# Moving the last eight query steps of the fourth batch from the second attention slot to the first

## The chip, the cores and the metric

The kernel runs on one core of a Trainium2 chip. The metric is the device time of one execution in microseconds (us), lower is better. In the texts PE is TensorE (matmuls), PEld its loading of weights, DVE is VectorE, ACT is ScalarE, POOL is GpSimd, and SP is SyncE, whose queue issues nearly all transfers (DMAs). In the profile's counts one matmul instruction on fp32 data appears as two records.

## The reference

One pre-normalised transformer block on fp32 data: 4 batches of 512 tokens, width 512, 32 query heads and 8 key/value heads of 16 columns, and a gated MLP of width 1376.

```python
x = L0_attn_resid                                   # (4, 512, 512)
x = x + _L0_attn_ref(_layernorm(x, axis=-1), Wq, Wk, Wv, Wo)
x = x + _L0_ffn_ref(_layernorm(x, axis=-1), W_gate, W_up, W_down)

# _L0_attn_ref
q = rope(resid @ Wq); k = rope(resid @ Wk); v = resid @ Wv      # rope: q*cos + rotate_half(q)*sin
att = where(causal, q @ k.T / 4, -inf); probs = softmax(att)
return concat_heads(probs @ v) @ Wo
# _L0_ffn_ref
return (silu(x @ W_gate.T) * (x @ W_up.T)) @ W_down.T
```

## The kernel before

**Groups and slots.** Attention is done in 32 groups, one for each batch, block of 8 heads (m = 0 to 3) and half of it (4 heads at a time). Eight groups make the slot of one batch: `slot(b, steps)` runs groups 8b to 8b + 7. `steps` is a list of other PE work, each entry with a planned cost, that is woven between the attention's products ("fill"). In the first slot the fill is the query, key and value projections of batches 1, 2 and 3. In the second slot it is what is left of batch 3's projections, then batch 0's output projection, LayerNorm and MLP. Slots three and four carry the later batches' MLPs.

**A group.** A group g has four visits (n = 0 to 3) and a last visit. In each visit PE makes score products of two kinds (lines 1014 and 1027): scores of group g + 2 in plain order, of which DVE takes the greatest of each row (`greatest`, line 1060, which writes the tile `low`), and scores of group g the other way round, of which ACT takes exponentials (line 1115). POOL zeroes what lies above the diagonal (`causal`, line 1120). PE may write the next visit's scores only after DVE and ACT have read this visit's. After the visits `last_visit` makes the last scores, ACT two exponentials, POOL two causal masks, and then POOL makes the masked queries of group g + 3 (`masked`, line 999). `averages` (line 1142) multiplies the exponentials with the values. The next group's first score products read a tile that line 999 writes.

**What fills the gaps.** After a visit's `greatest`, the call `odd_steps` lets DVE do small pieces that are due (rotations, transposes), and `gap(n)` then lets PE do fill steps up to a share of the slot's total: `part += total * shares[n] / 8`, and `fill` takes steps as long as half of the next one's cost still fits. In the first slot `shares` has four entries that matter, one for each visit.

**Projections.** `projected` makes a block of 128 rows by 512 tokens from 8 steps, one for each half of the tokens and each quarter of the depth: 4 instructions of 32 columns by 256 tokens (line 305), planned at 0.43 us. Steps 1 to 4 use tokens 0 to 255, steps 5 to 8 the others. `rest3` lists batch 3's 48 steps: keys 8, queries of block 0 8, values 8, queries of blocks 1, 2, 3 with 8 each. In the first slot ACT copies a finished block out of PSUM (line 357) and DVE and POOL rotate the copy: shuffle (line 364) and cosine product (line 368) on DVE, sine product (line 365) and sum (line 369) on POOL. In the second slot DVE reads PSUM itself. A finished key block also gets a shuffle on DVE (line 428) and four products on POOL (line 431), the "spread".

**LayerNorm of batches 2 and 3.** Twelve passes on ACT for each batch (`calm`, kinds a, b, c: lines 238 and 239, 245, 407), one popped in each `odd_steps` unless POOL work is being held; that is four in a group of the first slot. After each b pass POOL runs three small instructions (lines 246 to 248). After each c pass of batch 3 the tile is flipped: DVE transposes blocks of it (line 320), SP stores it in four DMAs (line 324) and loads it back in order as one of four tiles of `xnT` (line 326). The load of tile i - 1 is issued behind the stores of tile i; the last two loads come behind the stores of tile 3. The second slot's first products of batch 3 read that `xnT`, those of batch 2 another.

**POOL's other work in the first slot** is two sums in each group that prepare MLP weights (line 646), the scaling of the averages (line 1166), and rotations. POOL runs its instructions in the order in which they were issued.

**The MLP of one batch** (`seven`) makes ten units of seven half-size products each. The first product's result is kept in `once` (line 696), which lies in the last columns of the sine table; an ACT copy (line 734) writes it.

Of the kernel before, what the change touches and what calls it, by code (L numbers as in the profile page):

```python
# [18 lines left out]
B, T, D = 4, 512, 512  # L19
NH, NKV, DH = 32, 8, 16  # L20
FF = 1376
P = 128
NT = T // P
NK = D // P
# [50 lines left out]
def preln_block_kernel(  # L75
# [57 lines left out]
    rope_sb = const.tile([P, 2 * T + 4], F32, name="rope_sb")  # L133
# [11 lines left out]
    homes = [const.tile([P, NF, T], F32, name=f"home{n}") for n in range(3)] + [wd_sb]  # L145
# [17 lines left out]
    whole = NF - 1  # L163
# [19 lines left out]
    thin = [True]  # L183
# [67 lines left out]
    calm = deque()  # L251
# [373 lines left out]
    def after(step):  # L625
        return 0.0, step
# [64 lines left out]
    def seven(b, n, blocks):  # L691


        x, home = xnTs[0], homes[n]
        rights = (x[:, 0:2, 0 : 2 * P], x[:, 2:4, 0 : 2 * P], x[:, 2:4, 2 * P :], *((sums if b else sums0)[s] for s in (3, 0, 1, 2)))
        once = rope_sb[:, 2 * NK * 96 : 2 * T]
        carried = deque()

        def owed():
            if carried:  # L700
                carried.popleft()()

        def product(ps, right, w):
            for k in range(2):
                product_of(ps, w[:, k, :], rights[right - 1][:, k, :], k == 0, k == 1)

        def halved(t):
            return t.rearrange("p (h t) -> p h t", h=2)

        def unit(u):  # L710
            v, a, f = b * whole + u, u % 2, 2 * (u // 2)
            left, right = slice(0, 2 * P), slice(2 * P, T)
            out = (u_sb if a else home[:, f : f + 2, :]).rearrange("p f t -> p (f t)")
            corners = out.rearrange("p (h t) -> p h t", h=4)[:, 0:4:3, :]
            ps = {}

            def twice(t):
                return t.unsqueeze(1).broadcast_to([P, 2, 2 * P])

            def ended():  # L720
                for which in (1, 0):
                    g, t = home[:, f + which, :], u_sb[:, which, :]
                    if a == 0:
                        nc.scalar.activation(t, g, AF.Tanh, scale=0.5)  # L724
                        carried.append(lambda g=g, t=t: nc.vector.scalar_tensor_tensor(g, t, 1.0, g, ALU.add, ALU.mult))
                    else:
                        engine = nc.gpsimd if narrow[0] else nc.vector
                        engine.tensor_tensor(g, g, t, ALU.mult)  # L728

            def a1():  # L730
                load_blocks("y", v + 1)
                ps["a"] = bank()
                product(ps["a"][:, left], 1, place("a", v)[:, 0])
                nc.scalar.copy(once, ps["a"][:, left])

            def y1():
                load_blocks("v", v + 1)
                load_blocks("a", v + 1)
                ps["y"] = bank()
                product(ps["y"][:, left], 2, place("y", v)[:, 0])  # L740
                owed()

            def y2():
                product(ps["y"][:, right], 6, place("y", v)[:, 1])
                nc.vector.tensor_tensor(halved(out[:, T:]), halved(ps["y"]), twice(once), ALU.add)

            def v1():
                load_blocks("w", v + 1)
                ps["v"] = bank()
                product(ps["v"][:, left], 7, place("v", v)[:, 0])  # L750
                owed()

            def v2():
                product(ps["v"][:, right], 5, place("v", v)[:, 1])
                nc.vector.tensor_tensor(corners, halved(ps["v"]), twice(out[:, 3 * T // 2 :]), ALU.add)
                nc.vector.tensor_tensor(out[:, right], ps["v"][:, right], out[:, left], ALU.add)

            def w1():
                ps["w"] = bank()
                product(ps["w"][:, left], 4, place("w", v)[:, 0])  # L760

            def w2():
                product(ps["w"][:, right], 3, place("w", v)[:, 1])
                joined()

            def first_w2():
                ps["w"] = bank()
                product(ps["w"][:, right], 3, place("w", v)[:, 1])

            def last_w1():  # L770
                product(ps["w"][:, left], 4, place("w", v)[:, 0])
                joined()

            def joined():
                nc.vector.tensor_tensor(corners, halved(ps["w"]), corners, ALU.add)  # L775
                ended()

            order = (a1, y1, y2, v1, v2, w1, w2) if v else (a1, y1, first_w2, y2, v1, v2, last_w1)
            return [(0.86, step) for step in order]

        steps = []
        for u in range(whole):
            steps += unit(u)
            if u % 2 and b > 0:
                steps.append(after(lambda p=u // 2: later_sums(b, n, p, (0, 1))))
        t = [after(lambda s=s: sums_of(s, b)) for s in range(4)]
        ends = edge(n)
        if b == 0:
            return [*steps[:1], t[2], *steps[1:2], t[3], *steps[2:], *ends], t[:2]
        steps[12:12] = [after(moved)]  # L790
        for cut, step in zip((44, 50, 56, 62, 66, 72), blocks):
            steps.insert(cut, after(step))
        return [ends[0], t[0], ends[1], t[1], ends[2], t[2], ends[3], t[3], *steps]
# [400 lines left out]
    begin3, turned3, rest3, _ = projections(3, 3)  # L1194
    begin2, turned2, rest2, load2 = projections(2, 2)
    begin1, turned1, rest1, _ = projections(1, 1, then=load2)
# [68 lines left out]
    def slot(b, steps):  # L1265

        steps = deque(steps)
        total = sum(cost for cost, _ in steps)
        done, part = 0.0, 0.0
        groups = range(8 * b, 8 * b + 8)  # L1270
        thin[0] = copied[0] = b == 0
        narrow[0] = True

        shares = (0.2, 0.225, 0.2875, 0.2875, 0.0) if thin[0] else (0.19, 0.19, 0.22, 0.22, 0.18)

        def upcoming(n):

            upto, us = part + total * shares[n] / 8, 0.0
            for cost, _ in steps:
                if done + us + cost / 2 > upto:  # L1280
                    break
                us += cost
            return us

        def gap(n):
            nonlocal done, part
            part += total * shares[n] / 8
            pool_steps(sums_at(g)[n])
            done = fill(steps, part, done)

        for g in groups:
            h = g + 2
            if thin[0]:
                laid_out(g + 1)
            for n, visit in enumerate(visits):
                e = (e0, e0, e1, e1)[n]
                if h < len(GROUPS):
                    both_scores(h, g, visit)
                    exponentials(e[:, slice(0, 2) if n % 2 else slice(2, 4), :], less)
                elif n % 2 == 0:  # L1300
                    both_scores(h, g, visit)
                    exponentials(e[:, 2:4, :], less)
                    exponentials(e[:, 0:2, :], plain)
                if n == 1:
                    causal(e0, 0)
                if n == 3:
                    causal(e1, 0)
                    causal(e1, 3 * P, exchanged=True)
                all_greatest(h, visit)
                holding[0] = n == 3  # L1310
                if thin[0]:
                    odd_steps((1.3, 0.95, 0.95, 1.05)[n], (2, 1, 1, 0)[n])
                else:
                    odd_steps(min(0.8 * upcoming(n) - (0.4, 0.4, 0.8, 0.8)[n], 2.3))
                gap(n)
                if n == 1 and not thin[0]:
                    laid_out(g + 1)
            last_visit(h, g)
            turned_round(h)
            averages(g)  # L1320
            odd_steps(1.4)
            if not thin[0]:
                gap(4)
        thin[0] = copied[0] = narrow[0] = False
        emptied(len(full))
        if b == B - 1:
            do(later, len(later))
        for cost, step in steps:
            step()
# [10 lines left out]
        nc.scalar.dma_start(out=homes[1], in_=spill)  # L1340

    turns = [step for pair in zip(turned2, *[iter(rest1[-8:])] * 2) for step in pair]
    early = [*rest1[16:-8], *turns, begin3, *rest2, *turned3, *rest3[:-24]]
    for u in range(whole):
        early.insert(4 * u + 4, after(lambda u=u: copies(u)))

# [43 lines left out]
    def timed(steps, asides):  # L1390
# [15 lines left out]
        after(pack_rest),  # L1406
        after(lambda: pool_steps(0)),
        *blocks,
        *rest3[-24:-12],
        *before[1:],  # L1410
        *rest3[-12:-2],
        *behind,
        rest3[-2],
        first_sums[0],
# [76 lines left out]
```

## Time and profile before

| | us |
|---|---|
| median of 3 runs (lowest, highest) | 838.42 (837.94, 839.71) |
| the profiled execution | 838.44 |
| its span in the profile | 836.6 |
| PE busy in the span | 815.5 (97%) |
| DVE, POOL, ACT busy | 567.6, 369.1, 233.5 |
| chain that ended last | PE 78%, DVE 13%, issue 2%, DMA 2%, POOL 2% |

The chain that ended last is followed back from the last instruction, and its shares say which engine the end waited for. The first slot's group 0 ends at 65.62 us, groups 1 to 7 take from there to 173.64, and the second slot runs from 173.64 to 347.86. A group of the first slot takes 15.15 to 15.30 us, but for group 4 with 16.62 us. TensorE was granted its full clock in all of them (1.00 in the windows).

### The profile page before, as it was taken

Reading aid. Unit: us, or ns where it says so; the run is one execution under the profiler, and the core shown is the slowest. Engines: PE = TensorE matmul, PEld = TensorE weight load, DVE = VectorE, ACT = ScalarE, POOL = GpSimd, SP = SyncE. Lnnn points to the kernel's source line nnn. Section 1 sums busy time; section 2 is a strip of 40 time slices with the busy share of each in tenths; the row PEclk is TensorE's granted clock in tenths of the full one; section 3 lists DMA queues with packets and bytes.
Section 4 is the critical chain, followed back from the end, with each engine's and each line's share of the span. In section 5 each row is a group of like instructions: output and inputs, shape, how many; then the busy total and the mean of one; then the engine's idle time right before and its main releaser. Section 6 shows DMA issues by size and latency. Waiting matters only on the chain.

```text
span 836.6 us, 29336 instructions
## 1 busy us (share of the span) xinstructions
PE 815.5 (97%) x12460; PEld 469.6 (56%) x12460; DVE 567.6 (68%) x1635; ACT 233.5 (28%) x352; POOL 369.1 (44%) x524
## 2 busy tenths in 40 slices
PE   6999999999999999999999999999999999999998
PEld 5664454443555554333655555446555556788887
DVE  7976777878977774467777775687776633656632
ACT  1045654432323232122233332222332330011100
POOL 4576685873866333122365534522244435101130
PEclk9999999999999999999999999999999999999999
DMA  7544324152577640234244532234334434545901
GB/s 213 116 118 116 92 67 90 57 173 45 176 238 259 200 161 7 75 144 90 86 156 154 186 105 98 84 81 117 96 107 129 136 115 140 128 141 173 297 32 50
DMA packets 147857, 105.57 MB, mean 126 GB/s; under 512 B 60208, under 2 KB 133936, under 8 KB 147600
## 3 DMA queue, kind: packets, MB, share of 16 engines
q1 hardware_dynamic: 147008, 97.94, 39.8%
q10 hardware_dynamic: 720, 5.77, 1.7%
q8 instruction: 98, 1.61, 0.8%
q14 instruction: 31, 0.25, 0.1%
HBM read 82.25 MB, written 25.17 MB: 128 GB/s over the span
## 4 chain that ended last, share of the span: by engine, by line
PE 78%; DVE 13%; issue 2%; DMA 2%; POOL 2%; SPq 1%; ACT 1%; POOLq 0%; DVEq 0%; ACTq 0%
PE mm L305 38%; PE mm L302 15%; PE sc L1014 12%; DVE junk L1060 7%; PE av L1142 6%; PE sc L1027 4%; PE mm L596 2%; PE mm L588 1%; DVE st L222 1%; POOL e L1120 1%; DVE rot L364 1%; PE mm L310 1%; POOL qa L999 1%; DMA xa<-in_x 1%; ACT e L1115 1%
## 5 line engine op out<-in xcount | busy, mean ns | idle before, releaser
L1060 DVE CUSTOM_DVE_ANT_0 junk<-sc,mask 128x128 f32<-128x128 f32 (+3 forms) x512 | 251.1, 490 | 127.7 <-PE sc L1027 65.9
L1115 ACT ACTIVATE e<-sc 128x1024 f32<-128x1024 f32 (+1 forms) x192 | 165.5, 881 | 370.1 <-PE sc L1027 274.5
L305 PE MATMUL mm<-xnT,shared 128*32 128x256 f32 x3632 | 216.7, 381 | 0.0
L1120 POOL TENSOR_SCALAR_AFFINE_SELECT e<-e 128x512 f32<-128x512 f32 (+2 forms) x192 | 106.1, 562 | 198.2 <-ACT e L1115 195.2
L305 PEld LDWEIGHTS mm<-xnT,shared 128*32 128x32 f32 x3632 | 121.2, 110 | 86.1 <-issue 24.5
L1014 PE MATMUL sc<-home,qa 32*64 32x512 f32 (+6 forms) x2048 | 157.0, 421 | 6.4 <-DVE low L1060 3.2
L1027 PE MATMUL sc<-qa,home 32*64 32x512 f32 (+6 forms) x2048 | 152.4, 427 | 1.5 <-DVE low L1060 0.8
L1014 PEld LDWEIGHTS sc<-home,qa 32*64 32x64 f32 x2048 | 67.1, 131 | 82.3 <-DVE low L1060 29.3
L1142 PE MATMUL av<-e,home 128*32 128x512 f32 (+3 forms) x1024 | 82.6, 438 | 2.5 <-POOL e L1120 2.4
L302 PE MATMUL mm<-xnT,shared 128*128 128x256 f32 x360 | 80.2, 383 | 0.0
L302 PEld LDWEIGHTS mm<-xnT,shared 128*128 128x128 f32 x360 | 68.5, 192 | 11.6 <-issue 2.2
L305 PE MATMUL mm<-wd_sb,home 128*32 128x256 f32 (+3 forms) x848 | 71.2, 470 | 0.0
L1027 PEld LDWEIGHTS sc<-qa,home 32*64 32x64 f32 x2048 | 58.9, 130 | 20.9 <-DVE low L1060 7.2
L1142 PEld LDWEIGHTS av<-e,home 128*32 128x32 f32 x1024 | 30.6, 109 | 48.3 <-issue 35.0
L728 POOL TENSOR_TENSOR home<-home,u 128x512 f32<-128x512 f32 x30 | 37.9, 1282 | 28.4 <-DVE u L775 28.4
L305 PEld LDWEIGHTS mm<-wd_sb,home 128*32 128x32 f32 (+1 forms) x848 | 28.0, 110 | 36.9 <-issue 27.4
L305 PE MATMUL mm<-wo_sb,cx 128*32 128x512 f32 x384 | 45.4, 595 | 0.0
L818 POOL TENSOR_TENSOR wd_sb<-home 128x256 f32<-128x256 f32 x15 | 10.9, 729 | 74.4 <-DVE home L728 74.1
L1060 DVE DVE_READ_ACCUMULATOR2_ANT low<- 128x1 f32 x512 | 42.4, 83 | 0.0
L1166 POOL TENSOR_TENSOR inv<-us,inverse 128x256 f32<-128x256 f32 x32 | 21.7, 678 | 44.2 <-DVE inverse L1159 44.0
L724 ACT ACTIVATE u<-home 128x512 f32<-128x512 f32 x40 | 23.0, 622 | 62.9 <-DVE home L775 51.8
L225 POOL TENSOR_TENSOR rstd<-rstd,neghalf 128x1 f32<-128x1 f32 x24 | 15.6, 648 | 55.6 <-DVE rstd L224 55.6
(152 smaller groups left out, 928.4 us busy)
## 6 DMA issues: line engine op xcount, KB each, us to landing
shared<-packed SPq DMA_DIRECT2D x118, 256.0 KB
flip<-u SPq DMA_DIRECT2D x88, 64.0 KB
shared<-packed SPq DMA_DIRECT2D x40, 128.0 KB
xnT<-flip SPq DMA_DIRECT2D x18, 256.0 KB
wd_sb<-differences SPq DMA_DIRECT2D x7, 640.0 KB
rows<-in_x SPq DMA_DIRECT2D x14, 256.0 KB
out<-rows SPq DMA_DIRECT2D x13, 256.0 KB
xa<-in_x SPq DMA_DIRECT2D x12, 256.0 KB
```

Source lines behind the costliest of these rows:

```text
L302: nc.tensor.matmul(out, lhsT=lhsT, rhs=rhs, start=start, stop=stop)
L305: nc.tensor.matmul(out[c : c + 32], lhsT=lhsT[:, c : c + 32], rhs=rhs, start=start, stop=stop)
L596: nc.tensor.matmul(ps[96:P, ts(q, P)], lhsT=rest_w[:, a, kq, 32 * q : 32 * q + 32], rhs=xnTs[0][:, kq, most:], start=kq == 0, stop=kq == N ...
L724: nc.scalar.activation(t, g, AF.Tanh, scale=0.5)
L728: engine.tensor_tensor(g, g, t, ALU.mult)
L1014: nc.tensor.matmul(dst[at : at + 64, :n], lhsT=qa[g][rows_of(r), q : q + 64], rhs=keys_of(g)[rows_of(r), :n], start=True, stop=True,)
L1027: nc.tensor.matmul(dst[at : at + 64, first_q:], lhsT=keys_of(g)[rows_of(r), k : k + 64], rhs=qa[g][rows_of(r), P * j + first_q :], start=True,
L1060: nc.vector.tensor_tensor_reduce(out=junk[:, :n], in0=src, in1=mask[:, T - n : T] if i else mask[:, T:], scale=-1.0, scalar=BIG, op0=ALU.a ...
L1115: nc.scalar.activation(dst, src, AF.Exp, scale=1.0 / math.sqrt(DH))
L1120: nc.gpsimd.affine_select(out=e[rows, heads, c : c + P], in_=e[rows, heads, c : c + P], compare_op=ALU.is_ge, fill=0.0, base=base, pattern ...
L1142: nc.tensor.matmul(av[32 * r : 32 * r + 32, P * j :], lhsT=v[:, j, 4 * (m // 2) + r, DH * (1 - hf) : DH * (3 - hf)], rhs=e[:, r, c : c + n ...
L1166: nc.gpsimd.tensor_tensor(us[m][:, :, hf, :], turned[0][:, :, hf, :], by, ALU.mult)
```

## The change

Four places change; everything else is the same.

```diff
-        once = rope_sb[:, 2 * NK * 96 : 2 * T]
+        once = rope_sb[:, 2 * NK * 96 : 2 * T] if b else homes[0][:, whole, : 2 * P]
...
-        shares = (0.2, 0.225, 0.2875, 0.2875, 0.0) if thin[0] else (0.19, 0.19, 0.22, 0.22, 0.18)
+        shares = (0.22, 0.256, 0.262, 0.262, 0.0) if thin[0] else (0.19, 0.19, 0.22, 0.22, 0.18)
...
                 if thin[0]:
+                    if calm and n == 1:
+                        calm.popleft()()
                     odd_steps((1.3, 0.95, 0.95, 1.05)[n], (2, 1, 1, 0)[n])
...
-    early = [*rest1[16:-8], *turns, begin3, *rest2, *turned3, *rest3[:-24]]
+    early = [*rest1[16:-8], *turns, begin3, *rest2, *turned3, *rest3[:-16]]
...
-        *rest3[-24:-12],
+        *rest3[-16:-10],
         *before[1:],
-        *rest3[-12:-2],
+        *rest3[-10:-2],
```

- The eight steps of batch 3's query block 1 (`rest3[-24:-16]`) go from the head of the second slot's list to the end of the first slot's. The remaining sixteen stand differently around batch 0's output projection: six before it and ten behind, where twelve and twelve stood.
- The first slot's fill is shared out anew: more in visits 0 and 1, less in visits 2 and 3.
- In visit 1 of each group of the first slot one more LayerNorm pass is popped, so that a group pops five.
- For batch 0's MLP the kept product lies in row 10 of `homes[0]` and no longer in the sine table.

## The prediction

> **What bounds the kernel now.** I read the page first (PE busy 97%, the chain of waits 78% PE), then the busy times by group, because the change moves work between two stretches.
>
> ```profile
> core 0: us, PE busy (x) PEld busy (x) DVE busy (x) ACT busy (x) POOL busy (x), PEclk, DMA share, GB/s
> 96.21:111.46 15.25, 14.57 (x288) 7.21 (x288) 10.96 (x41) 9.16 (x18) 11.35 (x17) 1.00 0.02 4
> 111.46:128.08 16.62, 15.05 (x312) 7.49 (x312) 12.73 (x45) 8.56 (x14) 13.55 (x23) 1.00 0.32 83
> 173.64:347.86 174.22, 172.65 (x2981) 87.20 (x2984) 127.07 (x379) 50.85 (x70) 89.08 (x118) 1.00 0.47 147
> ```
>
> Each row gives a stretch, its length, and the busy time of each engine. Groups 3 and 4 of the first slot leave PE 0.68 and 1.57 us idle; the whole second slot leaves 1.57 us in 174. So a PE step taken out of the second slot should shorten it by its own length, and a step put into the first slot is free only where PE idles. Where it idles is seen in the timeline of PE in group 3:
>
> ```profile
> 96.38 0.65 PE L1014 MATMUL sc<-home,qa 32*64 32x512 f32 x2 [0.17 <-POOL qa L999]
> ...
> 97.74 1.50 PE L305 MATMUL mm<-xnT,shared 128*32 128x256 f32 x24
> 99.34 0.65 PE L1014 MATMUL sc<-home,qa 32*64 32x512 f32 x2
> ...
> 100.39 1.50 PE L305 MATMUL mm<-xnT,shared 128*32 128x256 f32 x24
> 102.06 0.54 PE L1014 MATMUL sc<-home,qa 32*64 32x384 f32 x2 [0.17 <-DVE low L1060]
> ...
> 103.01 1.93 PE L305 MATMUL mm<-xnT,shared 128*32 128x256 f32 x32
> 105.07 0.54 PE L1014 MATMUL sc<-home,qa 32*64 32x384 f32 x2
> ```
>
> A row is start, length, line and what ended an idle time. Visits 0, 1 and 2 start at 96.38, 99.34 and 102.06, so they last 2.96, 2.72 and 3.01 (visit 3 also 3.01). Each ends when DVE has taken the greatest values. The fill of three steps (24 records, 1.50) or four (32, 1.93) is nearly done by then: a step is 0.43, and there is under 0.25 of room. The last stretch of a group hangs on POOL:
>
> ```profile
> 107.81 1.91 POOL L1120 TENSOR_SCALAR_AFFINE_SELECT e<-e 128x512 f32<-128x512 f32 x3
> 109.94 0.83 POOL L1120 TENSOR_SCALAR_AFFINE_SELECT e<-e 128x256 f32<-128x256 f32 x2 [0.22 <-ACT e L1115]
> 110.87 0.70 POOL L999 TENSOR_SCALAR qa<-home,rope_sb 128x512 f32<-128x512 f32 x1
> ```
> ```profile
> 121.68 1.52 POOL L431 TENSOR_SCALAR home<-kr,rope_sb 128x512 f32<-128x512 f32 x2
> 123.17 1.52 POOL L431 TENSOR_SCALAR home<-ks,rope_sb 128x512 f32<-128x512 f32 x2
> 124.64 2.75 POOL L1120 TENSOR_SCALAR_AFFINE_SELECT e<-e 128x512 f32<-128x512 f32 x5
> 127.50 0.69 POOL L999 TENSOR_SCALAR qa<-home,rope_sb 128x512 f32<-128x512 f32 x1
> ```
>
> The first is group 3, the second group 4. PE's last scores start at 108.08 and 123.28, the queries (L999) 2.79 and 4.22 later. In group 4 the key spread of batch 2 holds the masks back: 1.43 lost, which is why that group takes 16.62. Five masks take 2.75, so POOL must be free by 0.05 after the last scores start.
>
> **The change part by part.** The time is made against the profiled execution, 838.44, which is the median's 838.42 within 0.02. Which fill stands in which visit I counted in the built programs' order.
>
> *Second slot, steps removed.* Fills of 48 and 16 records there take 2.80 and 1.07, so four steps are 1.73 and eight are 3.46. Gain 3.46. Their DVE and POOL work hardly moves: the block finishes at the very end of the first slot, and its rotation lands in group 8. There one more cosine product (0.69) stands in front of the first greatest; visit 1 starts at 178.02, 0.11 behind DVE's end, so this costs some 0.5. In group 10 PE waited 0.19 for DVE and 0.41 for POOL's last masks; the two gate products that held these up (L728, 2.53) now stand a visit earlier: gain 0.5. I set the two against each other: 0 (bounds -0.7 to +1.0). The new place of `once` takes away one ACT wait of 2.4 us for POOL's sine product, but PE had other work and waited for nothing then: 0. PE idles 0.6 in groups 9 to 11 together, and the two waits of group 10 are all of it, so nothing is left to gain.
>
> *First slot, fill too long for its visit.* A fill starts 1.36 behind visit 0's start, 1.05 behind visit 1's, 0.95 behind the others', and the next scores start 0.07 before it ends. Four steps in visit 0 give 1.36 + 1.93 - 0.07 = 3.22 against 2.96: 0.26, in groups 1, 3 and 5: 0.78. Four steps in visit 1 give 2.91 against 2.72: 0.2, in group 6 (group 4 is counted below). Group 2 gets a transpose and three steps (2.09 to 2.23) in visit 1, where a transpose and two steps (1.66) stood: 3.14 against 2.73, 0.41, and 0.04 in visit 0; group 1's visit 2 gets the same pair, 3.11 against 3.01: 0.1. Four steps in visits 2 and 3 end at 2.81 of 3.01 and cost nothing. Group 0's longer visit 1 hides under that group's own POOL backlog (masks at 62.19, 0.6 behind its last scores); cover gone, 0.2. Sum 1.53 (1.1 to 1.9).
>
> *First slot, POOL.* The moved steps bring batch 3's LayerNorm and both key spreads forward. Group 4: after visit 1's start POOL now has a sine product (begins at 0.67, 1.80), a sum 1.27, a weight sum 0.73, a mask 0.64, a LayerNorm trio (104.53 to 105.80 in group 3, 1.3 with its gaps), the spread 3.0, another weight sum 0.73 and another trio 1.3 ahead of the masks: free at 11.5. The last scores come at 2.91 + 3.01 + 3.01 = 8.93. So the masks are 2.5 late, and the group takes 2.96 + 11.5 + 2.75 + 0.8 = 18.0 against 16.62: 1.4. Group 3: counted from visit 0's start, DVE's cosine product lets POOL's sum run 3.6 to 4.9, then weight sum to 5.6, mask 6.2, trio (behind ACT's pass) 7.75, sine product 9.05, weight sum 9.75, trio 11.1, key sum 12.4, with the last scores at 3.22 + 2.7 + 6.02 = 11.95: 0.4. Group 7 gets batch 3's spread, with no trio: 11.8 against 11.7, 0.1. Sum 1.9 (0 to 3.4). The fifth pass itself is 0.8 to 1.0 on ACT, whose exponential of visit 2 has 0.75 of slack: 0.
>
> On the sine product: its length in the trace is 1.27 to 1.81, long where a DVE cosine product (0.69) runs beside it.
>
> ```profile
> L365 POOL TENSOR_TENSOR rot<-rot,rope_sb x18: 1267/1288/1808, 37.0 to 215.9; 128x512 f32<-128x512 f32 x18
> ```
>
> The Trainium skill, SBUF — State Buffer, section "SBUF: two separate sides", says that VectorE with two SBUF inputs and GpSimd contend for one port pair as an exclusive lock, held for the whole instruction. The rows show 0.52 of lengthening beside an operation of 0.69, so nearly that; by the page group 4 would be 0.17 later still and the total as much higher, by the row it stays as summed.
>
> *First slot, a tile that is not there yet.* SP's timeline of the flips in group 5, and a load of such a tile in the chain of waits:
>
> ```profile
> 135.02 2.25 SPq L324 DMA_DIRECT2D flip<-u  x4
> 137.38 1.33 SPq L326 DMA_DIRECT2D xnT<-flip  x1
> 138.75 2.25 SPq L324 DMA_DIRECT2D flip<-u  x4
> 141.12 3.52 SPq L326 DMA_DIRECT2D xnT<-flip  x2
> ```
> ```profile
> 25.85 2.71 DMA wd_sb<-flip
> ```
>
> Before, batch 3's first key step came at 147.41 in group 6, ten us behind tile 1's load. Now it stands in visit 3 of group 5, while tile 2's flip is still the odd piece of visit 1, and tile 1's load is queued on SP behind tile 2's stores. From visit 2's start: transpose 0.71, stores 2.2 to 2.4, load 2.71, together 5.7. The step comes at 3.01 + 0.95 + 0.64 = 4.6. It waits 1.1, PE with all behind it, less 0.2 of room in the visit: 0.9. Lower bound 0 (a load that need not wait for its own stores may land sooner than the chain's), upper 1.9 (the load of 137.38 took 0.8 longer to issue). Tiles 2 and 3 are due after that wait and then just arrive.
>
> Sum: -3.46 + 0 + 1.53 + 1.9 + 0.9 = +0.9, so 839.3.
>
> **Rivals.** *POOL is later still (slower).* In groups 3, 4 and 7 POOL is the last; if there its sine products take 1.80 each (0.5 more in groups 3 and 7) and its weight sums 1.18, as the one at 152.69 did (0.45 more: once in group 3, twice in group 4), the POOL term is 2.4 larger: 841.7. It decides from the point where POOL is free 0.05 behind the last scores; for it speaks that POOL is busy 13.55 of 16.62 in group 4, against it that sums mostly take 0.73. *POOL is in time (faster).* The spread of batch 2 starts a visit earlier than before; if trios and sums find room in front of it, group 4 loses nothing and the old 1.43 goes: -3.46 + 1.53 - 1.4 + 0.9 = -2.4, 836.0. For it speaks that groups 5 and 6 carry two rotations and two weight sums and are in time (masks at 155.07, last scores at 155.10), against it the count above. *The second slot doesn't give the steps back.* Its weight sums, stores and loads run at a set number per group; if these hold the MLP's first units, half of 3.46 comes: 841.1. Against it: PE never waits for a load there.
>
> **How the numbers follow.** Chances: the forecast 0.38, POOL later 0.28, POOL in time 0.24, second slot 0.10. 0.2% (1.68 us) is about what a measurement of this kernel can tell from no change, so no change ends at 836.8 and 840.1. Of the forecast a quarter lies above 840.1 (its own range is 838.0 to 840.9) and 0.02 of it below 836.8; of POOL later 0.95, of the second slot 0.8 are slower; of POOL in time two thirds are faster. Slower 0.10 + 0.27 + 0.08 = 0.44 rounded, faster 0.16 + 0.01 = 0.17, the same 0.39. All bounds at once give 835.4 to 843.2; 8 in 10 I put at 836.3 to 842.4.
>
> **What would show it.** The second slot some 3.5 shorter than 174.22; group 4 near 18.0, with masks 2.5 behind its last scores; group 5 some 1.2 longer than 15.15, PE waiting for a DMA ahead of a key step in visit 3; groups 1, 2, 3 and 6 longer by 0.2 to 0.7. Wrong would be a first slot that takes as long as before, or a second one that keeps its length.

## The result, and the profile after

The changed kernel takes 840.38 us (median of 17 runs, 839.21 to 842.34), the kernel before 839.46 in its 17 runs beside them (837.94 to 840.66). The medians are 0.92 apart; the ratio, taken run beside run, is 1.0018, 95% interval 1.0011 to 1.0025: 1.5 us slower, 0.9 to 2.1. The profiled execution took 840.51, with a span of 838.8 against 836.6.

The first view is the busy time by stretch after the change, for groups 3, 4, 5 and the second slot.

```profile
core 0: us, PE busy (x) PEld busy (x) DVE busy (x) ACT busy (x) POOL busy (x), PEclk, DMA share, GB/s
96.94:113.03 16.09, 15.64 (x328) 8.09 (x328) 11.50 (x42) 9.86 (x19) 12.20 (x19) 1.00 0.02 4
113.03:131.16 18.13, 15.39 (x288) 6.97 (x288) 12.93 (x43) 9.75 (x17) 14.12 (x23) 1.00 0.44 106
131.16:147.81 16.65, 15.06 (x281) 7.11 (x280) 11.59 (x38) 6.95 (x9) 6.09 (x12) 1.00 0.40 82
178.30:348.97 170.67, 167.94 (x2916) 84.53 (x2920) 125.00 (x375) 50.90 (x70) 83.66 (x113) 1.00 0.48 150
```

The second slot fell from 174.22 to 170.67, by 3.55. Group 4 now leaves PE 2.74 us idle, group 5 1.59. The table has the lengths of the groups (a group ends where its averages, line 1142, end), and beside them those of three experiments told below.

| us | before | after | e1 | e5 | e7 |
|---|---|---|---|---|---|
| group 1 | 15.29 | 15.55 | 15.54 | 15.55 | 15.54 |
| group 2 | 15.30 | 15.84 | 15.85 | 15.84 | 15.85 |
| group 3 | 15.25 | 16.09 | 16.09 | 16.08 | 16.10 |
| group 4 | 16.62 | 18.13 | 15.58 | 15.43 | 15.43 |
| group 5 | 15.15 | 16.65 | 16.77 | 15.47 | 15.47 |
| group 6 | 15.26 | 15.33 | 15.33 | 15.50 | 15.33 |
| group 7 | 15.15 | 15.16 | 15.15 | 15.14 | 15.15 |
| groups 1 to 7 | 108.02 | 112.75 | 110.32 | 109.03 | 108.86 |
| second slot | 174.22 | 170.67 | 170.68 | 170.69 | 169.16 |

Groups 1 to 7 lost 4.73 and the second slot won 3.55. Group 0 was 0.07 shorter, so at the end of group 31 the changed kernel is 1.11 behind (698.77 against 697.66). The rest of the difference between the two profiled spans, 1.04, comes from one wait in the last MLP, which the list of PE's waits there shows with 0.9:

```profile
PE mm L302 <- DMA shared<-packed: 0.9, 1, 0.9
```

The columns are the time in all, how often, and the longest. The trace of before has no such wait, but nothing was changed in that stretch, and the experiments show it as 0, 0.3, 0.4 or 0.7. It varies from one execution to the next.

**Group 1.** PE's timeline in visit 0, which now has four steps (32 records):

```profile
65.72 0.64 PE L1014 MATMUL sc<-home,qa 32*64 32x512 f32 x2 [0.17 <-POOL qa L999]
...
67.08 1.93 PE L305 MATMUL mm<-wd_sb,shared 128*32 128x256 f32 x32
68.94 0.65 PE L1014 MATMUL sc<-home,qa 32*64 32x512 f32 x2
```

The visit lasts 3.22, and visit 1's scores start where the fill ends. Before, with three steps, it lasted 2.96 (65.78 to 68.74).

**Group 4.** POOL's timeline, and PE's at the start of visit 1 and from the last scores on:

```profile
116.83 1.81 POOL L365 TENSOR_TENSOR rot<-rot,rope_sb 128x512 f32<-128x512 f32 x1 [2.04 <-DVE rot L364]
...
122.72 1.52 POOL L431 TENSOR_SCALAR home<-kr,rope_sb 128x512 f32<-128x512 f32 x2
124.22 1.52 POOL L431 TENSOR_SCALAR home<-ks,rope_sb 128x512 f32<-128x512 f32 x2
125.70 0.73 POOL L646 TENSOR_TENSOR wo_sb<-wo_sb 128x256 f32<-128x256 f32 x1
...
127.73 2.75 POOL L1120 TENSOR_SCALAR_AFFINE_SELECT e<-e 128x512 f32<-128x512 f32 x5
130.58 0.69 POOL L999 TENSOR_SCALAR qa<-home,rope_sb 128x512 f32<-128x512 f32 x1
```
```profile
116.16 0.64 PE L1014 MATMUL sc<-home,qa 32*64 32x512 f32 x2
...
125.07 0.69 PE L1027 MATMUL sc<-qa,home 32*64 32x256 f32 x16 [0.56 <-DVE low L1060]
...
128.43 0.85 PE L1142 MATMUL av<-e,home 128*32 128x384 f32 x8 [1.34 <-POOL e L1120]
129.70 1.46 PE L1142 MATMUL av<-e,home 128*32 128x128 f32 x16 [0.42 <-POOL e L1120]
```

The masks (line 1120) start 2.66 behind the last scores (125.07), where before it was 1.36, and PE's averages wait for them twice.

**Group 5.** PE's timeline in visit 3, and SP's queue:

```profile
141.19 0.64 PE L305 MATMUL mm<-xnT,shared 128*32 128x256 f32 x8
142.99 1.50 PE L305 MATMUL mm<-xnT,shared 128*32 128x256 f32 x24 [1.17 <-DMA xnT<-flip]
144.42 0.68 PE L1027 MATMUL sc<-qa,home 32*64 32x256 f32 x16
```
```profile
137.83 1.95 SPq L324 DMA_DIRECT2D flip<-u  x4
139.82 0.51 SPq L326 DMA_DIRECT2D xnT<-flip  x1
```

The first 8 records are the last query step; the 24 behind the wait are three key steps. The load that they need (tile 1, at 139.82) was issued behind the four stores of tile 2.

**Group 8.** DVE, POOL and PE at the start of the second slot:

```profile
179.69 0.63 DVE L368 TENSOR_TENSOR wd_sb<-wd_sb,rope_sb 128x512 f32<-128x512 f32 x1
...
181.03 1.55 DVE L368 TENSOR_TENSOR wd_sb<-wd_sb,rope_sb 128x512 f32<-128x512 f32 x1
182.50 0.68 DVE L1060 CUSTOM_DVE_ANT_0 junk<-sc,mask 128x512 f32<-128x512 f32 x1
```
```profile
180.75 1.28 POOL L369 TENSOR_TENSOR wd_sb<-wd_sb,rot 128x512 f32<-128x512 f32 x1
```
```profile
183.98 0.64 PE L1014 MATMUL sc<-home,qa 32*64 32x512 f32 x2 [1.46 <-DVE low L1060]
```

Two cosine products stand ahead of the first greatest (182.50), and the second takes 1.55 where the first took 0.63: it starts while POOL's sum runs (to 182.03) and ends 0.55 behind it. PE waits 1.46.

### The profile page after: what moved, and what is told of

Read it like the earlier page. It is cut to its first block, busy times and chain, and to the rows that moved or that the text cites. A ratio compares the mean times of both kernels' runs of the same rounds, so it can differ in the third digit from the quotient of the medians.

```text
span 838.8 us, 29340 instructions
## 1 busy us (share of the span) xinstructions
PE 814.8 (97%) x12460; PEld 468.5 (56%) x12460; DVE 567.3 (68%) x1635; ACT 234.6 (28%) x353; POOL 368.6 (44%) x524
## 4 chain that ended last, share of the span: by engine, by line
PE 79%; DVE 10%; POOL 4%; DMA 2%; issue 2%; SPq 1%; ACT 1%; POOLq 0%; DVEq 0%; ACTq 0%
PE mm L305 37%; PE mm L302 16%; PE sc L1014 12%; PE av L1142 6%; DVE junk L1060 6%; PE sc L1027 4%; PE mm L596 2%; DMA shared<-packed 1%; POOL e L1120 1%; PE mm L588 1%; DVE st L222 1%; ACT e L1115 1%; POOL qa L999 1%; PE mm L310 1%; DVE u L320 0%
```

## The experiments

Each time is a median; each ratio is to the kernel before on the same chip. Chips differ (medians of the kernel before: 839.09, 840.43, 840.30 and 840.05), so kernels of different chips are compared by their ratios and group lengths, not their times. e1 to e4 ran on one chip, e5 to e8 on a second, e9 to e11 on a third, e12 on a fourth.

**e1: the spread later.** `soon` holds a step back for a number of `odd_steps` calls.

```diff
-                last = spread if early else lambda: soon.append((1, (0.75, spread)))
+                last = spread if early else lambda: soon.append((5 if b == 2 else 1, (0.75, spread)))
```

> The changed kernel, with batch 2's key spread (3.0 us on POOL) held until group 5's start instead of standing ahead of group 4's masks. Theory (POOL's list ahead of group 4's masks makes the group long): POOL is free before the last scores of group 4 start, the group goes from 18.13 to about 15.5, the sum is -2.6: about 837.9, 0.3% under the changed kernel and 0.2% under the one before. Rival (the group is long because its fill is too long for PE): group 4 stays above 17.5 and the time stays at 840.4. Rival (the spread only moves its wait): group 5 grows by 1 to 2.5 us and the time stays above 839.5.

Measured: 837.95, ratio 0.9984 (0.9975 to 0.9993). POOL in group 4, where the last scores start at 126.17:

```profile
125.84 1.92 POOL L1120 TENSOR_SCALAR_AFFINE_SELECT e<-e 128x512 f32<-128x512 f32 x3
...
129.65 1.52 POOL L431 TENSOR_SCALAR home<-kr,rope_sb 128x512 f32<-128x512 f32 x2
```

POOL is ready ahead of the last scores and makes the spread behind the next queries. Group 4 gives back 2.55, group 5 takes 0.13. So it was POOL's list, not PE's fill, that made group 4 longest, and the spread doesn't only move its wait.

**e2: every tile's load ahead of the next tile's stores.**

```diff
+        def back(a):
+            nc.sync.dma_start(out=dst[:, :, ts(a, P)], in_=flip[n].rearrange("(k p) t -> p k t", p=P)[:, :, ts(a, P)])
+
+        if i > 0:
+            back(i - 1)
...
-        for a in [i - 1, i] if i == last else [i - 1] if i > 0 else []:
-            nc.sync.dma_start(out=dst[:, :, ts(a, P)], in_=flip[n].rearrange("(k p) t -> p k t", p=P)[:, :, ts(a, P)])
+        if i == last:
+            back(i)
```

> The changed kernel, with each flipped tile's load given to SP ahead of the next tile's stores instead of behind them. Theory (PE waits in group 5 because tile 1's load is queued behind tile 2's stores): the wait of 1.17 ahead of the key step in visit 3 of group 5 goes, the group goes from 16.64 to 15.2 to 15.5, the sum is -1.2: about 839.2. Rival (the load is late because the transfer itself is slow, not because of the queue): the wait stays above 0.6 and the time within 0.5 of 840.4. Rival (what PE saves in group 5 it loses in group 6, where tiles 2 and 3 are due): group 6 grows by about 1 and the time stays at 840.4.

Measured: 842.17, ratio 1.0044 (1.0032 to 1.0057): slower than the change alone. Group 5 did give back 1.18 (15.47), but group 6 took 0.66 (15.99), and the list of PE's waits in the last MLP has a new line. Lines behind the edit have numbers higher by 6; on SP, L324 is now the load and L330 the stores. SP's queue in groups 5 and 6, PE's new wait, and SP's own waits for stores from 118 to 160 us, in e2 and then in the change:

```profile
138.46 1.96 SPq L330 DMA_DIRECT2D flip<-u  x4
142.09 0.38 SPq L324 DMA_DIRECT2D xnT<-flip  x1
142.56 2.86 SPq L330 DMA_DIRECT2D flip<-u  x4
147.16 0.38 SPq L324 DMA_DIRECT2D xnT<-flip  x1
```
```profile
PE mm L602 <- DMA xnT<-flip: 1.3, 1, 1.3
```
```profile
SPq L324 <- DMA flip<-u: 4.7, 5, 1.5
```
```profile
SPq L326 <- DMA flip<-u: 1.1, 2, 0.8
```

The load of tile 2 is next in SP's queue at 140.42 and starts at 142.09: it waits until its own tile's stores have landed, and the stores of tile 3 wait behind it. Put behind the next tile's stores, as the change has it, the loads wait 1.1 in all and not 4.7. The third expectation, a loss in group 6, came with two thirds of its size. The last MLP's flips lost more, which no theory had named: what follows group 31 takes 141.55 in e2's profile and 138.98 in e1's.

**e3: both.**

> The changed kernel with both edits. If the two losses are separate: -2.6 and -1.2 add up to about 836.6. If the group-5 wait comes back because group 4's end no longer gives the tiles time (the first key step then stands 2.6 us earlier, but so do the flips, which follow the same visits), about 837.9 as with the spread alone.

Measured: 839.74, ratio 1.0008 (0.9999 to 1.0017); neither number. Group 4 is 15.43 and group 5 15.46, so the two gains do add up, but group 6 takes 16.56 with a tile's wait of 1.2, and the last MLP's wait for a flipped tile is 0.9.

**e4: the kernel before, with the spread held.** The edit of e1 with 4 for 5.

> The kernel before, with batch 2's key spread held until group 5's start. Theory: its group 4 loses the 1.43 us by which the masks were late, 16.62 to 15.2, total about 837.0 to 838.0 (-1.4 against the kernel before of the same chip). Then e1's gain is only partly a repair of what the change did: 1.4 of its 2.6 was there before. Rival: group 5 takes the spread's 3.0 us as a wait: no change or slower.

Measured: 837.36, ratio 0.9981 (0.9972 to 0.9990). Its group 4 is 15.22, group 5 15.30. So 1.4 of what e1 wins was to be had without the change, and with this repair on both sides the changed kernel is not faster: 837.95 (e1) against 837.36. This trace also has the unchanged second slot once more: 173.67. Group 11 takes 21.65 there and 22.10 in the trace of before, from the same code.

**e5: e1, and the load of tile 1 alone ahead.** The condition `thin[0]` holds in the first slot and also in the opening before it, where one more flip changes its order; the later flips keep theirs.

```diff
+        back = lambda a: nc.sync.dma_start(out=dst[:, :, ts(a, P)], in_=flip[n].rearrange("(k p) t -> p k t", p=P)[:, :, ts(a, P)])
...
+        if ahead := thin[0] and i == 2: back(1)
...
-        for a in [i - 1, i] if i == last else [i - 1] if i > 0 else []:
+        for a in [] if ahead else [i - 1, i] if i == last else [i - 1] if i > 0 else []:
+            back(a)
```

> The changed kernel with the key spread held until group 5 (as in e1), and with the load of tile 1 alone, in the first slot alone, given to SP ahead of tile 2's stores. Theory (the queue order makes PE wait in group 5, and e2 lost elsewhere, in group 6 by 0.66 and in the last MLP by 1.3, where a load that is issued at once waits on SP for its own tile's stores): group 5 goes from 16.77 to 15.4, group 6 stays at 15.33, the last MLP has no wait for a flipped tile, total about 836.6 (-1.3 against e1). Rival (the SP queue as such is short of time there, so that any gain in group 5 comes back in group 6): 837.9 as e1.

Measured: 836.89, ratio 0.9958 (0.9945 to 0.9970). SP's queue (L318 is the load):

```profile
134.16 0.45 SPq L318 DMA_DIRECT2D xnT<-flip  x1
135.84 4.99 SPq L324 DMA_DIRECT2D flip<-u  x8
140.99 3.17 SPq L318 DMA_DIRECT2D xnT<-flip  x2
```

PE in visit 3 of group 5, now four steps in a row and then the last scores:

```profile
139.19 1.93 PE L305 MATMUL mm<-xnT,shared 128*32 128x256 f32 x32
141.25 0.68 PE L1027 MATMUL sc<-qa,home 32*64 32x256 f32 x16
```

Group 5 is 15.47, 1.30 under e1's, and PE waits for no tile. Group 6 is 15.50, 0.17 over e1's; e7, with the same order, has 15.33 again. The queue's order, not how full it is, was the cause.

**e6: e1, and a sixth pass per group** (`if calm and n in (1, 2)`).

> The changed kernel with the spread held as in e1 and a sixth LayerNorm pass in each group (one more in visit 2), queue order as in the change. Theory (the tile is late because its LayerNorm pass is): three flips move into group 4, no wait for a tile is left, group 5 goes to about 15.4; but batch 2's spread now falls between group 6's masks and its last scores, where it costs 0 to 1 us: total 836.6 to 837.6. Rival (POOL or ACT cannot take six passes in groups 1 to 5): groups 1 to 3 grow by 0.5 or more in all and the time stays at or above 837.9.

Measured: 837.77, ratio 0.9964 (0.9950 to 0.9978). No wait for a tile is left, and group 3 is 15.50, not longer. But the spread fell ahead of group 5's masks, not group 6's as expected: that group's averages take 3.42 instead of 2.44, and the group 16.84. The tiles can also be had in time through earlier passes, and then POOL is late again.

**e7: e5, and rotations not forced out at the slot's end.**

```diff
-        emptied(len(full))
+        emptied(len(full) if b else 0)
```

> e5, and at the end of the first slot the rotations that are still owed are left in their list instead of being forced ahead of group 8's first greatest. Theory (two cosine products ahead of the first greatest, the second of them held up to 1.55 us while POOL's sum runs, make PE wait 1.46 in group 8): the wait goes, group 8 from 20.98 to about 19.5 to 19.8, total 1.2 to 1.4 under e5, about 835.3. Rival (the DVE work is only put off, and group 9, whose wait is 0.5, takes it over): within 0.4 of e5.

Measured: 835.55, ratio 0.9942 (0.9930 to 0.9955). DVE in group 8:

```profile
176.36 0.69 DVE L1060 CUSTOM_DVE_ANT_0 junk<-sc,mask 128x512 f32<-128x512 f32 x1
...
177.71 0.69 DVE L368 TENSOR_TENSOR wd_sb<-wd_sb,rope_sb 128x512 f32<-128x512 f32 x1
```

The greatest values come first, the wait of 1.46 is gone, and group 8 goes from 20.99 to 19.46; group 9 keeps its 21.72. This version beats both kernels. Against e4, the kernel before with the spread repaired, its groups 1 to 15 take 278.02 and not 280.33: with most of the collisions out of the way, moving the steps, with the shares and the fifth pass that came along, is worth 2.3 of the 3.46. The edits of e5 and e7 were not run on the kernel before; in e4's profile PE has neither of the waits that they remove.

**e8: the kept product back in the sine table.** In this kernel the product's copies overwrite sines that batch 3's last query rotation still reads, so some of batch 3's queries are not the reference's.

```diff
-        once = rope_sb[:, 2 * NK * 96 : 2 * T] if b else homes[0][:, whole, : 2 * P]
+        once = rope_sb[:, 2 * NK * 96 : 2 * T]
```

> The changed kernel with the MLP's kept product back in the sine table's last columns. If the new place is worth nothing, as the prediction has it: within 0.4 of the changed kernel's 840.4. Rival (ACT's copy waiting for POOL's sine products holds up the MLP's first units): 0.5 to 1.5 us slower, with groups 10 to 12 longer.

Measured: 840.85, ratio 1.0006 (0.9995 to 1.0016), no slower than the change. ACT's first copy and POOL's last sine product:

```profile
217.12 0.37 ACT L734 COPY rope_sb<-mm 128x256 f32<-128x256 f32 x1 [0.31 <-PE mm L305]
```
```profile
222.01 1.28 POOL L365 TENSOR_TENSOR rot<-rot,rope_sb 128x512 f32<-128x512 f32 x1
```

The new place is worth nothing in time; it is there because the remaining steps now stand behind the MLP's first units.

**e9: e7, with group 3's two weight sums in group 5.**

```diff
-            return (1, 1, 0, 0, 0) if g < 8 else (3, 2, 2, 0, 3)
+            return {3: (0, 0, 0, 0, 0), 5: (2, 2, 0, 0, 0)}.get(g, (1, 1, 0, 0, 0)) if g < 8 else (3, 2, 2, 0, 3)
```

> e7 with group 3's two weight sums (0.73 and 1.18 us on POOL) run in group 5 instead. Theory (POOL is 0.68 late for group 3's masks, so its averages take 3.18 instead of 2.44): the averages take 2.44 to 2.5, group 3 goes from 16.10 to 15.4, group 5 keeps 15.47; -0.7 against e7, about 834.8. Rival (group 3 is long by its fill and DVE): group 3 stays above 15.9, time as e7.

Measured: 839.48, ratio 0.9988 (0.9978 to 0.9997). Group 3 went to 15.49 as expected, but group 5 to 20.44. Its POOL and SP:

```profile
141.75 1.54 POOL L646 TENSOR_TENSOR wo_sb<-wo_sb 128x256 f32<-128x256 f32 x2 [6.50 <-DMA wo_sb<-in_wg]
```
```profile
133.39 0.45 SPq L649 DMA_DIRECT2D packed<-wo_sb  x1
137.60 0.95 SPq L179 DMA_DIRECT2D wo_sb<-in_wg  x2
138.59 0.51 SPq L318 DMA_DIRECT2D xnT<-flip  x1
```

A sum brings its store and the next weights' load with it. Here the load waits on SP for that store (137.60), tile 1's load stands behind it (138.59), and PE's key step waits 3.5. A moved POOL step had moved two queues. The wait explains 3.5 of the 5.0 by which group 5 is longer than e7's. Behind it TensorE was granted a lower clock. The first row is e9, the second the changed kernel in the same two microseconds; the clock is the third figure from the right:

```profile
core 0: us, PE busy (x), PEclk, DMA share, GB/s
144.00:146.00 2.00, 2.00 (x40) 0.50 0.65 131
```
```profile
144.00:146.00 2.00, 2.00 (x52) 1.00 0.60 168
```

The three key steps behind the wait take 2.00 instead of 1.50.

**e10: e7 without the fifth pass.**

> e7 without the fifth LayerNorm pass of a group. Theory (the pass is there so that the tiles come in time for the moved steps): tile 0 flips in group 4, tiles 1 to 3 in group 5's visits 1 to 3; the key step in visit 3 of group 5 waits 2.5 to 3.5 us for tile 1 and group 6's visit 0 another 1 to 2 for tile 3; 3 to 5 us over e7, 838.5 to 840.5. Rival (four passes leave POOL and ACT lighter, and the tiles are in time anyway): as e7 or faster by up to 1.

Measured: 841.84, ratio 1.0018 (1.0009 to 1.0028), by the ratios 6.4 over e7, where 3 to 5 was expected. PE's waits in groups 1 to 7:

```profile
PE mm L310 <- ACT xa L407: 2.7, 2, 1.4
PE mm L305 <- DMA xnT<-flip: 2.6, 1, 2.6
```

The key step's wait is as expected, the one of tile 3 did not come. Two things were not expected: batch 2's transposes in group 2 wait twice for ACT's c pass, 2.7 in all, and behind the key step's wait the granted clock falls as in e9 (0.50 from 146 to 148 us), so that group 5 takes 3.9 more than in e7. The fifth pass is needed at both ends.

**e11: e9 with the old shares** (0.2, 0.225, 0.2875, 0.2875).

> e9 with the old shares of the first slot's fill (0.2, 0.225, 0.2875, 0.2875). Theory (a visit lasts as its greatest values need, and each fill longer than its room adds its excess): no visit 0 has four steps any more and group 2 has a transpose and two steps at most in visits 0 and 1, so groups 1, 2, 3 and 5 give back 0.06, 0.5, 0.06 and 0.06, and the fill sums up to about 0.7 less: 834.0 to 834.3. Rival (what is taken out of visits 0 and 1 overfills visits 2 and 3, or POOL's later sine product in group 3 takes it back): as e9 or slower.

Measured: 840.05, ratio 0.9998 (0.9989 to 1.0007). Groups 1 and 2 give back 0.07 and 0.43 (in group 1 visit 0 gives back 0.26, and the fourth step in visit 1 takes 0.2), but group 3 goes from 15.49 to 16.60: a second sine product of 1.80 now falls into it, and POOL is late again. The rival holds: the new shares overfill group 2 and keep POOL free in group 3.

**e12: e7, with one of group 3's sums in group 2.**

```diff
-            return (1, 1, 0, 0, 0) if g < 8 else (3, 2, 2, 0, 3)
+            return {2: (1, 2, 0, 0, 0), 3: (1, 0, 0, 0, 0)}.get(g, (1, 1, 0, 0, 0)) if g < 8 else (3, 2, 2, 0, 3)
```

> e7 with one of group 3's two weight sums (the 1.18 one) run in visit 1 of group 2, where POOL idles 1.22 us ahead of the next sine product; the order of SP's queue is that of e7, so that no weight load comes closer to its sum than there. Theory (e9's loss was the load that four sums in one group run into, and its gain in group 3 was POOL's): group 3 goes from 16.10 to 15.5, all other groups keep e7's lengths, about 834.9. Rival (a sum moved ahead holds up group 2): group 2 grows by 0.3 or more and the time stays within 0.3 of e7.

Measured: 835.72, ratio 0.9950 (0.9936 to 0.9964). Group 3 is 15.40, group 2 stays at 15.84, but the time is not told apart from e7's, whose interval overlaps: 0.7 in one group is less than two chips differ. Groups 1 to 15 take 277.46, 0.56 under e7's.

## Why the prediction was right

It said 839.3, 0.9 over its profiled execution, as the sum of a gain and three losses. The kernel before took 839.46 in the runs beside the change and not 838.42, so the figure to compare is the difference: 1.5 (0.9 to 2.1) in the runs, and 1.11 at the end of group 31 in the two profiles. The gain and the three losses were found where they were put, each with a part of its sum off:

- *Second slot, -3.46.* Measured -3.55, or -3.00 against e4's trace of the same code. The sum hides two errors in "other effects, 0". Group 8 was put at 0.5 and waits 1.46, because the prediction counted the extra cosine product at 0.69 and it took 1.55. Group 9 waits 0.47 that was not foreseen. Against that, group 10's two waits (0.60) went as said, and group 11's 0.45 is there in one execution and not in another. PE's busy time fell by 4.71 (172.65 to 167.94); the steps are 3.46 of it and group 11's 0.45, and the remaining 0.8 stays open. That 3.55 lies so near 3.46 is therefore in part luck.
- *Fill too long, +1.53.* Groups 1 and 2 lost 0.26 and 0.54 (0.36 and 0.45 were said), group 6 0.07 (0.2), group 5 without its wait (e5) 0.32 (0.26), group 3 without the late POOL (e12) 0.15 (0.26): 1.34. The cause is the one said: with four steps visit 0 of group 1 lasts 3.22, the sum's own figure, and in e11 with three steps 2.96. The 0.1 for group 1's visit 2 did not come (3.00 there).
- *POOL, +1.9.* Group 4 lost 1.51 (1.4 was said), with POOL's list as counted: the sine product 0.67 behind visit 1's start (116.16), the masks 11.57 behind it (11.5 was said). In e1, without the wait for POOL, the group is still 0.36 over e4's 15.22: the longer fill, which the wait hides. Group 3 lost 0.69 (16.09 less e12's 15.40; 0.4 was said), group 7 0.01 (0.1): 2.2. e1 shows that POOL is the cause in group 4, e9 and e12 in group 3, where the sum of 1.18 of the rival "POOL later still" did come (105.89 in the change), while its sine product of 1.80 did not (1.30).
- *A tile not there yet, +0.9.* PE waited 1.17, and e5 gave it all back (1.30 against e1). The tile came when it was said to: the step starts 5.76 behind visit 2's start (137.23; 5.7 was said). The room of 0.2 was there too: in e5 the four steps of that visit end at 141.12, where scores that wait for nothing else would start 0.07 earlier, and the last scores start at 141.25. The term that was mis-sized is the step's place, 3.01 + 0.95 + 0.64 = 4.6. The 0.64 is what the profile shows for one step by itself (141.19), but the steps of a row follow each other in 0.43. With 0.43 the place is 4.39, the step 1.3 late, and less 0.2 of room that is 1.1.
- *`once` and the fifth pass, 0.* e8 and the trace agree on `once`. Of the pass the prediction weighed only its own length; e10 shows that without it two other waits come.

So groups 1 to 7 lost 4.73 where 4.33 was said, and the second slot gave 3.55 where 3.46 was said. Of the rivals, "POOL in time" is what e1 makes by another order, "POOL later still" came with one sum in group 3, and "the second slot doesn't give the steps back" is out.

## What to carry to other kernels

A step moved into a full stage brings everything that must be ready for it: here eight matmul steps pulled LayerNorm passes, a key spread, flips and their DMAs forward, and these cost more than the steps themselves did there (2.2 for POOL and 1.2 for the tile against 1.3). List what each engine and each DMA queue has to finish ahead of the stage's last wait, in issue order, before you count the step itself; then change that order, since e7's three edits remove no work and took back 5.4 us in groups 1 to 15 (283.42 to 278.02), of which 1.4 had nothing to do with the change (e4). Where a load reads what a store has just written, put other transfers between the two (e2), but none that makes the load late (e5).

## What the runs showed of the hardware

- A load of data that earlier stores write held SP's queue until they had landed: in e2 1.67 passed between the end of the stores' issue (140.42) and the load's start (142.09), with all later transfers behind it.
- A DVE product of two operands in SBUF, 0.63 to 0.69 alone, took 1.55 when POOL's sum was running as it came. The prediction had weighed only the other direction, POOL waiting for DVE, though the trace of before has such a product too (1.31 at 151.96, 0.55 of it behind the end of POOL's sine product at 152.72). The Trainium skill, SBUF — State Buffer, section "SBUF: two separate sides", says that whichever of the two starts first holds the shared ports for its whole instruction. The row agrees: 0.28 behind the sum's start, 1.00 until its end, and then 0.55, a little less than the product takes alone.
- After a wait of PE of 2.6 to 3.5 the granted clock fell: to 0.50 in 144 to 146 us of e9 (wait of 3.5), to 0.55 there in e11 (3.1), to 0.50 in 146 to 148 of e10 (2.6). After the waits of 1.17 in the change and 1.29 in e1 it stayed at 1.00. So a long wait cost up to 1.5 more than its own length.
- Executions of one code differ by more than one would think: group 0, which is the same in the change, e1 and e8, took 65.55, 66.49 and 66.38, and the wait for weights in the last MLP is listed with 0 to 0.9. Differences under 1 us are read from groups, not from spans.
